# Sixteen-head attention: the four zero products of a half step, each on a column tile of 32, written as one product over the full array

## The chip, the cores and the metric

The kernel runs on one core of a Trainium2 chip. The metric is the device time of one execution in microseconds (us). The engines are named as in the profile: PE is TensorE (matrix products), PEld its weight loads, DVE is VectorE, ACT is ScalarE, POOL is GpSimd, SP issues DMAs. The profile also gives the TensorE clock that was granted, as a share of full speed.

## What is computed

A residual network of sixteen layers on `x` of shape (1, 2048, 128): in turn an attention or state-space layer and a feed-forward layer, each as `x = x + f(layernorm(x))`. The change touches the three layers of softmax attention with 16 heads of 8 columns:

```python
def heads(W, b):                       # 16 heads of 8
    y = jnp.einsum('btc,oc->bto', x, W) + b
    return y.reshape(B, T, H, D).transpose(0, 2, 1, 3)
att = jnp.einsum('bhqd,bhkd->bhqk', q, k) * (1.0 / np.sqrt(D))
att = jax.nn.softmax(att, axis=-1)     # L0_attn_b: after rope, and under a causal mask
y = jnp.einsum('bhqk,bhkd->bhqd', att, v)
return jnp.einsum('btc,oc->bto', y.transpose(0, 2, 1, 3).reshape(B, T, C), Wp) + bp
...
x = x + _L0_attn_b_ref(_layernorm(x, axis=-1), ...)   # stage Causal
...
x = x + _L2_attn_b_ref(_layernorm(x, axis=-1), ...)   # stage Attn2
...
x = x + _L3_attn_b_ref(_layernorm(x, axis=-1), ...)   # stage Filtered: q and k are filtered by a learned mask
```

## The kernel before

**Stages.** The layers are stages, one after the other: `CumSum, Moe0, Causal, Moe0, Mamba, Mla, Ssm, Moe2, Attn2, Moe2, Hale, Moe3, Filtered, Moe3`. While one stage ends, the first blocks of the next are fed in. A scheduler that goes by a simulated timeline orders the instructions of all stages up to Attn2; for the PE instructions of the 16-head stages it has no choice, because the helper `in_turn` stamps each of them with its place in the order of issue.

**Units.** `Causal`, `Attn2` and `Filtered` are of the class `Attn16`. The 2048 tokens are four blocks `b` of 512 queries, and the 16 heads are four groups `g` of four. A unit is a pair (g, b), so a stage has 16 units. For a unit there are two passes over the keys:

- `pass_a` finds the maximum of each query's scores. Line 829 multiplies 128 queries by 512 keys for two heads (`ps_a`, 128 x 1024), each head on a row tile of 32 rows; DVE takes the maximum over each row of 512 (line 833, `at_mx`). `set_max` puts the negated maxima into two spare rows of `q` (transposes of line 850, an ACT copy, a DMA).
- `pass_b` makes the scores the other way round. For each tile `kt` of 128 keys, in two halves `jj` of two heads each, line 900 multiplies keys by queries (row tiles of 32, `ps_b`), ACT takes the exponential (line 906, `at_P`), and `av` multiplies the values by it.

**The half step.** `pass_a` runs ahead of `pass_b`, and for each half `jj` PE gets, in this order: two products of line 829, two of line 900, and one call of `av`. I call this a half step. `av(kt, off, ps, half)` does one half of the query columns of tile `kt`, so the call in the first half step of a tile needs the exponentials of the tile before, and the second call needs nothing new. A stage without a mask has 512 half steps, `Causal` has 320 (keys beyond the diagonal are left out).

**The call of av.** `self.acc` (`ps_c`, one bank of PSUM) collects the output of the unit's four heads, each on 32 partitions. Line 879 is four products, one for each head `j`, of 128 rows and 32 columns of weights (`at_V`) on the column tile `32 * j`, with 256 columns of `at_P` in fp32; each shows in the trace as two matmul records (two passes). Then come the products with zeros (line 883):

```python
z = s if kt == 0 or end < BW else slice(half * BW // 2, (half + 1) * BW // 2)
for j in (3, 2, 1, 0):
    if not (kt == nkt - 1 and half):
        self.in_turn(nc.tensor.matmul(self.acc[32 * j : 32 * j + 32, z], c.zerob, c.wide[:, z], start=False, stop=False))
```

`zerob` is a constant tile of zeros (line 64), `wide` one of ones. The products add zero to `acc`. They have the same form as the value products, 128 rows on column tiles of 32, but are bf16. The last half step of a unit has none: 1296 of the 1344 half steps have four.

**Buffers.** `ps_a` has two buffers of two banks, `ps_b` three banks, `ps_c` one; these are the eight banks of PSUM. PE takes its instructions in order; the DMAs of these stages (maxima into `q`) go by SP's queue.

**The end of a unit.** After the last call of `av`, ACT copies `acc` to `at_u` (line 888). Every second unit ends with `tail` (transposes over the full array, line 922), and every fourth with `out` (transposes and the output product, lines 940 and 946). `prep` makes the next unit's `q` (line 760, row tiles) and once per block the projection for the next block's heads.

Of the kernel before, what the change touches and what calls it, by code (L numbers as in the profile page):

```python
# [15 lines left out]
BF16 = mybir.dt.bfloat16  # L16
# [5 lines left out]
P = 128  # L22
# [10 lines left out]
class Core:  # L33
    def __init__(self, ctx, tc, ins):
        self.ctx, self.tc, self.nc, self.ins = ctx, tc, tc.nc, ins
        nc = self.nc
        self.per = ctx.enter_context(tc.tile_pool(name="per", bufs=1))
        self.x = self.per.tile([P, NT, P], F32, name="x")
        self.load_x(ins["x"])
        self.ident = self.per.tile([P, P], F32, name="ident")  # L40
        make_identity(nc, self.ident)
        self.identb = self.per.tile([P, P], BF16, name="identb")
        nc.vector.tensor_copy(self.identb, self.ident)
        self.identr = self.per.tile([P, P], F32R, name="identr")
        nc.vector.tensor_copy(self.identr, self.ident)
        self.ones = self.per.tile([P, P], F32, name="ones")
        nc.vector.memset(self.ones, 1.0)
        self.nhalf = self.per.tile([P, 4], F32, name="nhalf")
        nc.vector.memset(self.nhalf, -0.5)
        self.rev8 = self.per.tile([P, 4, E], F32, name="rev8")  # L50
        for e in range(E):
            nc.vector.memset(self.rev8[:, :, e : e + 1], float(E - e))
        self.neg01 = self.load(self.per, "neg01", (P, 1), ins["neg01"])
        slots = self.per.tile([P, 4, P], F32R, name="slots")
        with tc.tile_pool(name="st0", bufs=1) as st:
            nc.vector.tensor_copy(slots, self.load(st, "slots_raw", (P, 4, P), ins["slots"]))
        self.slots = {"q": (slots[:, 0], slots[:, 1]), "k": (slots[:, 2], slots[:, 3])}
        self.kone = self.load(self.per, "kone", (P, 1), ins["kone"])
        one = self.per.tile([2, 1], F32R, name="ones2")
        nc.vector.tensor_copy(one, self.ones[0:2, 0:1])  # L60
        self.ones2 = one.to_broadcast([2, BW])
        self.wide = self.per.tile([P, BW], BF16, name="wide")
        nc.vector.memset(self.wide, 1.0)
        self.zerob = self.per.tile([P, 32], BF16, name="zerob")
        nc.vector.memset(self.zerob, 0.0)
        self.psum = ctx.enter_context(tc.tile_pool(name="psum", bufs=1, space=PSUM))
        self.shared = {}
# [617 lines left out]
class Attn16(Attention):  # L685
# [175 lines left out]
    def pass_b(self, u, scale):  # L861
        c, nc = self.c, self.c.nc
        g, b, i0, i1 = u
        self.turn_due(u)
        q, KT = self.qb[(g, b)], self.KT[g]
        nkt = 4 * b + i1 if self.causal else NT
        end = i1 * P

        def av(kt, off, ps, half):


            if kt == i0 == g % 2 == half == 0:
                self.acc = c.ps("c")
            mid = (off + end) // 2
            s = slice(mid, end) if half else slice(off, mid)
            for j in (3, 2, 1, 0):
                h = 27 * (4 * (g // 2) + j) + 9 * (g % 2)
                start, stop = kt == i0 == g % 2 == half == 0, kt == nkt - 1 and g % 2 == half == 1
                self.in_turn(nc.tensor.matmul(self.acc[32 * j : 32 * j + 32, s], self.V[:, kt, h : h + 32], ps[j][:, s], start=start, stop=stop))  # L879
            z = s if kt == 0 or end < BW else slice(half * BW // 2, (half + 1) * BW // 2)  # L880
            for j in (3, 2, 1, 0):
                if not (kt == nkt - 1 and half):
                    self.in_turn(nc.tensor.matmul(self.acc[32 * j : 32 * j + 32, z], c.zerob, c.wide[:, z], start=False, stop=False))  # L883
            if kt == nkt - 1 and half:
                self.closed = u
            if kt == nkt - 1 and g % 2 == half == 1:
                self.u = self.wk.tile([P, BW], F32, name="at_u", tag="at_t", bufs=2)
                nc.scalar.copy(self.u, self.acc)  # L888

        for kt in range(nkt):  # L890
            off = max(i0, kt - 4 * b) * P if self.causal else i0 * P
            diag = self.causal and kt >= 4 * b + i0
            ps = []
            for jj in range(2):
                self.pair = 1 - jj
                yield (kt + (jj + 1) / 2) / nkt
                pbs = [c.ps("b") for _ in range(2)]
                for k in range(2):
                    r = rows(2 * jj + k)
                    self.in_turn(nc.tensor.matmul(pbs[k][:, off:end], KT[r, kt * P : (kt + 1) * P], q[r, off:end], start=True, stop=not diag))  # L900
                if diag:
                    for k in range(2):
                        self.in_turn(nc.tensor.matmul(pbs[k][:, off : off + P], c.identb, self.maskbT, start=False, stop=True))
                for k in range(2):
                    p = self.wk.tile([P, BW], F32, name="at_P", bufs=self.NP)
                    nc.scalar.activation(p[:, off:end], pbs[k][:, off:end], AF.Exp, scale=scale)  # L906
                    ps.append(p)
                self.turn_due()
                self.later(1)
            self.late += [partial(av, kt, off, ps, half) for half in range(2)]  # L910
# [76 lines left out]
def rows(j):  # L987
    return slice(32 * j, 32 * j + 32)
# [1450 lines left out]
```

## Time and profile before

| | |
|---|---|
| median of 3 runs | 4835.98 us (4833.01 to 4851.77) |
| profiled execution | 4842.59 us, of which the span from first to last instruction is 4840.6 us |
| mean granted TensorE clock | 0.922 |
| PE, DVE, ACT busy | 91%, 77%, 63% of the span |
| half steps of Causal | from 345 to 855 us in the span, 1.60 us each on average |
| half steps of Attn2 | from 2214 to 2874 us, 1.29 us each |
| half steps of Filtered | from 3950 to 4617 us, 1.30 us each |
| records of line 883 | 5184 matmuls and 5184 weight loads |

The profile is one execution, so sums are held against its own 4842.59 us; the median lies 6.6 us lower. A matmul's recorded duration contains a part that overlaps with the next one, so costs are read from the distance between starts, not from durations.

### The profile page before, as it was taken

What the parts mean: (1) busy time and instruction counts of PE and PEld (TensorE: products, weight loads), DVE (VectorE), ACT (ScalarE), POOL (GpSimd) and SP (SyncE); (2) the same over time, 40 slices, a digit from 0 to 9 for tenths busy, and PEclk for the clock granted to TensorE, in tenths of its full rate; (3) what the DMA queues carried; (4) which work ended last, traced back from release to release, by engine and by line L of the source; (5) the groups of instructions that cost most, each with busy time, mean ns of one, the idle gap of its engine ahead of it and who ended that gap; (6) DMA issues with size and microseconds to landing.
All of it is one profiled execution on the core that took longest, in us unless ns stands there. A gap on an engine that the chain in (4) does not pass through costs nothing.

```text
span 4840.6 us, 89173 instructions
## 1 busy us (share of the span) xinstructions
PE 4411.5 (91%) x36388; PEld 2496.4 (52%) x36388; DVE 3713.6 (77%) x5694; ACT 3052.4 (63%) x5570; POOL 947.6 (20%) x826
## 2 busy tenths in 40 slices
PE   6979999988799998799999999989988989999998
PEld 4744444655344443463444457656656634444466
DVE  7867886689666653789999958457768879999777
ACT  4634667775355555356888875345546648888876
POOL 4730000544100000330000013012215600000056
PEclk9966899998699999888999999889998969999999
DMA  1010000000000000000000000112211000000000
GB/s 52 6 45 6 4 2 9 22 1 17 17 14 14 18 14 4 8 1 2 2 2 2 2 4 12 33 50 51 51 48 37 9 8 2 2 2 2 2 20 7
DMA packets 69484, 73.33 MB, mean 15 GB/s; under 512 B 17616, under 2 KB 44102, under 8 KB 69076
## 3 DMA queue, kind: packets, MB, share of 16 engines
q1 hardware_dynamic: 69076, 67.64, 5.0%
q8 instruction: 287, 4.70, 0.4%
q14 instruction: 121, 0.99, 0.1%
HBM read 32.09 MB, written 1.05 MB: 7 GB/s over the span
## 4 chain that ended last, share of the span: by engine, by line
PE 68%; DVE 21%; ACT 5%; issue 3%; POOL 2%; DMA 1%; SPq 0%; POOLq 0%; ACTq 0%; DVEq 0%
PE ps_c L879 15%; PE ps_a L829 10%; PE ps_c L1483 5%; DVE at_mx L833 4%; PE ps_b L900 4%; PE ps_a L1443 3%; PE ps_c L883 3%; PE ps_b L1496 3%; PE ps_b L148 2%; PE ps_a L148 2%; PE ps_a L150 2%; PE ps_b L149 2%; PE ps_a L149 2%; PE ps_b L150 2%; DVE m_hl L455 1%
## 5 line engine op out<-in xcount | busy, mean ns | idle before, releaser
L906 ACT ACTIVATE at_P<-ps_b 128x512 f32<-128x512 f32 (+2 forms) x2688 | 1414.4, 581 | 335.0 <-PE ps_b L900 211.1
L833 DVE TENSOR_REDUCE at_mx<-ps_a 128x2 f32<-128x1024 f32 (+2 forms) x1344 | 1537.7, 1184 | 106.5 <-PE ps_b L900 66.8
L879 PE MATMUL ps_c<-at_P,at_V 128*32 128x256 f32 (+3 forms) x10752 | 868.3, 396 | 7.8 <-ACT at_u L888 7.3
L900 PE MATMUL ps_b<-at_q,at_KT 32*128 32x512 f32 (+2 forms) x2688 | 759.5, 499 | 6.6 <-DMA at_q<-at_mT 5.0
L829 PE MATMUL ps_a<-at_KT,at_q 32*128 32x512 f32 (+3 forms) x2688 | 701.1, 521 | 48.0 <-DVE at_mx L833 45.7
L829 PEld LDWEIGHTS ps_a<-at_KT,at_q 32*128 32x128 f32 x2688 | 267.1, 196 | 497.4 <-issue 338.1
L1444 DVE TENSOR_REDUCE ml_mx<-ps_a 128x2 f32<-128x1024 f32 x256 | 305.4, 1222 | 216.4 <-PE ps_a L1443 215.4
L454 ACT ACTIVATE m_hh<-ps_a,moe_b 128x512 fp32r<-128x512 f32 x512 | 349.8, 689 | 189.1 <-DVE m_h L451 158.0
L455 POOL TENSOR_TENSOR m_hl<-m_h,m_hh 128x512 fp32r<-128x512 f32 x256 | 360.5, 1409 | 541.1 <-ACT m_hh L454 529.3
L1498 ACT ACTIVATE ml_P<-ps_b 128x512 f32<-128x512 f32 (+1 forms) x544 | 272.5, 576 | 231.8 <-PE ps_b L1496 229.7
L879 PEld LDWEIGHTS ps_c<-at_P,at_V 128*32 128x32 f32 x10752 | 215.8, 110 | 359.2 <-issue 181.0
L883 PE MATMUL ps_c<-wide,zerob 128*32 128x256 bf16 x5184 | 391.1, 282 | 0.0
L266 POOL TENSOR_TENSOR ln_rs<-ln_ve,nhalf 128x4 f32<-128x4 f32 x56 | 61.8, 1104 | 1650.3 <-DVE ln_ve L264 1641.4
L900 PEld LDWEIGHTS ps_b<-at_q,at_KT 32*128 32x128 f32 x2688 | 326.3, 189 | 73.5 <-issue 44.2
L455 DVE TENSOR_TENSOR m_hl<-m_h,m_hh 128x512 fp32r<-128x512 f32 x256 | 257.1, 1005 | 79.4 <-ACT m_hh L454 77.9
L453 ACT ACTIVATE m_h<-ps_a,moe_b 128x512 f32<-128x512 f32 x320 | 220.6, 690 | 77.1 <-DVE m_hl L455 42.0
L1483 PE MATMUL ps_c<-ml_P,ml_V 128*33 128x512 f32 (+3 forms) x1088 | 257.5, 596 | 2.9 <-ACT ml_P L1498 2.9
L148 PE MATMUL ps_b<-m_hh,moe_w2h 128*128 128x512 f32 x512 | 221.7, 433 | 20.7 <-DVE m_t L475 17.8
L149 PE MATMUL ps_b<-m_hl,moe_w2h 128*128 128x512 f32 x512 | 213.9, 418 | 26.4 <-DVE m_hl L455 20.7
L148 PE MATMUL ps_a<-ln_h,moe_w1h 128*128 128x512 f32 x512 | 218.7, 428 | 10.7 <-ACT m_hh L454 10.6
L883 PEld LDWEIGHTS <-zerob 128*32 128x32 bf16 x5184 | 156.1, 100 | 113.6 <-issue 10.8
L149 PE MATMUL ps_a<-ln_l,moe_w1h 128*128 128x512 f32 x512 | 207.4, 405 | 0.0
(655 smaller groups left out, 7759.7 us busy)
## 6 DMA issues: line engine op xcount, KB each, us to landing
hl_KS<-hl_pkh SPq DMA_DIRECT2D x160, 64.0 KB
moe_w_raw<-in_l0f_W SPq DMA_DIRECT2D x32, 256.0 KB
ml_pad<-ml_QT SPq DMA_DIRECT2D x32, 256.0 KB
moe_w_raw<-in_l3f_W SPq DMA_DIRECT2D x32, 256.0 KB
hl_KS<-hl_pkl SPq DMA_DIRECT2D x80, 64.0 KB
at_pad<-at_q SPq DMA_DIRECT2D x64, 64.0 KB
at_q<-at_mT SPq DMA_DIRECT2D x192, 4.0 KB
at_cosT<-in_cosT SPq DMA_DIRECT2D x8, 256.0 KB
```

The source lines that it names most:

```text
L148: nc.tensor.matmul(out, lh, rh, start=start, stop=False)
L149: nc.tensor.matmul(out, lh, rl, start=False, stop=False)
L454: nc.scalar.activation(hh, ph, AF.Relu, bias=bias)
L455: (nc.gpsimd if f in ((0, 2) if self.spare else MS) else nc.vector).tensor_tensor(hl, h, hh.bitcast(F32), ALU.subtract)
L829: self.in_turn(nc.tensor.matmul(pa[:, k, :w], q[r, i * P : (i + 1) * P], KT[r, ch * BW : ch * BW + w], start=True, stop=True))
L833: nc.vector.tensor_reduce(mx[:, i, 2 * jj : 2 * jj + 2, ch], pa[:, :, :w], AX.X, ALU.max)
L879: self.in_turn(nc.tensor.matmul(self.acc[32 * j : 32 * j + 32, s], self.V[:, kt, h : h + 32], ps[j][:, s], start=start, stop=stop))
L883: self.in_turn(nc.tensor.matmul(self.acc[32 * j : 32 * j + 32, z], c.zerob, c.wide[:, z], start=False, stop=False))
L900: self.in_turn(nc.tensor.matmul(pbs[k][:, off:end], KT[r, kt * P : (kt + 1) * P], q[r, off:end], start=True, stop=not diag))
L906: nc.scalar.activation(p[:, off:end], pbs[k][:, off:end], AF.Exp, scale=scale)
L1444: nc.vector.tensor_reduce(mx[:, i, :, ch], pa, AX.X, ALU.max)
L1483: self.in_turn(nc.tensor.matmul(self.acc[64 * j : 64 * j + m, s], v, ps[k][j][:, s], start=kt + k == 0, stop=kt + k == NT - 1))
```

## The change

The four products with zeros become one product with 128 columns of weights, over all 128 partitions of `acc` and the same query columns. The tile of zeros grows from 32 to 128 columns. It is for all three 16-head stages, since they share `pass_b`; `Hale` has its own `pass_b` without such products.

```diff
-        self.zerob = self.per.tile([P, 32], BF16, name="zerob")
+        self.zerob = self.per.tile([P, P], BF16, name="zerob")
         nc.vector.memset(self.zerob, 0.0)
...
             z = s if kt == 0 or end < BW else slice(half * BW // 2, (half + 1) * BW // 2)
-            for j in (3, 2, 1, 0):
-                if not (kt == nkt - 1 and half):
-                    self.in_turn(nc.tensor.matmul(self.acc[32 * j : 32 * j + 32, z], c.zerob, c.wide[:, z], start=False, stop=False))
+            if not (kt == nkt - 1 and half):
+                self.in_turn(nc.tensor.matmul(self.acc[:, z], c.zerob, c.wide[:, z], start=False, stop=False))
```

In the instruction streams PE loses 3 x 1296 matmuls and as many weight loads. The order of the other PE instructions within the half steps is as before. From Causal to Attn2 the scheduler exchanges some neighbouring instructions on DVE, ACT and POOL, and outside the half steps a few dozen on PE; SP's order is the same. The line numbers behind the change fall by one.

## The prediction

> **What bounds the kernel now.** I read the page first: where PE's clock falls, and what carries the chain.
>
> ```profile
> PEclk9966899998699999888999999889998969999999
> PE ps_c L879 15%; PE ps_a L829 10%; PE ps_c L1483 5%; DVE at_mx L833 4%; PE ps_b L900 4%; PE ps_a L1443 3%; PE ps_c L883 3%; PE ps_b L1496 3%; PE ps_b L148 2%; PE ps_a L148 2%; PE ps_a L150 2%; PE ps_b L149 2%; PE ps_a L149 2%; PE ps_b L150 2%; DVE m_hl L455 1%
> L883 PE MATMUL ps_c<-wide,zerob 128*32 128x256 bf16 x5184 | 391.1, 282 | 0.0
> ```
>
> The zero products are on the chain (3%), and never wait. The clock is low in slices 3 and 4 (Causal) and where stages change. Then the timeline inside Filtered, two half steps at full clock:
>
> ```profile
> 4400.79 0.64 PE L879 MATMUL ps_c<-at_P,at_V 128*32 128x256 f32 x8
> 4400.93 2.19 ACT L906 ACTIVATE at_P<-ps_b 128x512 f32<-128x512 f32 x4 [0.19 <-PE ps_b L900]
> 4401.25 0.29 PE L883 MATMUL ps_c<-wide,zerob 128*32 128x256 bf16 x4
> 4401.47 0.18 PEld L829 LDWEIGHTS ps_a<-at_KT,at_q 32*128 32x128 f32 x2 [0.32 <-issue]
> 4401.48 0.59 PE L900 MATMUL ps_b<-at_q,at_KT 32*128 32x512 f32 x2
> 4402.07 0.16 PEld L879 LDWEIGHTS ps_c<-at_P,at_V 128*32 128x32 f32 x8 [0.31 <-ACT at_P L906]
> 4402.53 0.29 PE L883 MATMUL ps_c<-wide,zerob 128*32 128x256 bf16 x4
> 4402.75 0.49 PE L829 MATMUL ps_a<-at_KT,at_q 32*128 32x512 f32 x2
> ```
>
> The value products start at 4400.79, zeros .46 later, scores .22 after that. The first half step, 4400.37 to 4401.48, is PE alone: 1.11 us. In the second, L879 waits for ACT until 4402.07 (PE was ready .43 after 4401.47, so .17 are slack), and ACT's first exponential had waited for PE (.19). So two half steps are one ring of 2.39: scores on PE, ACT until 4402.07, then values and zeros, 0.68. Only one of two zero groups lies in it. DVE's maxima follow PE.
>
> **What a zero product costs, and a change of tile shape.** The timeline again, at a unit's end, where there are no zeros, and at other changes of shape:
>
> ```profile
> 2253.85 0.64 PE L879 MATMUL ps_c<-at_P,at_V 128*32 128x256 f32 x8
> 2254.41 0.50 PE L829 MATMUL ps_a<-at_KT,at_q 32*128 32x512 f32 x2
> ```
> ```profile
> 3252.65 0.29 PE L2144 MATMUL ps_b<-hl_am,hl_V 128*32 128x128 f32 x4
> 3252.88 0.49 PE L2157 MATMUL ps_a<-hl_QP,hl_KS 128*128 128x512 f32 x1
> ```
> ```profile
> 3081.53 0.28 PE L1929 MATMUL ps_b<-at_mc,identb 128*128 128x256 bf16 x1
> 3081.74 0.43 PE L1918 MATMUL ps_c<-at_P,at_V 128*32 128x64 f32 x16
> ```
>
> From values to scores takes .56 without zeros and .68 with: the four cost .11, one stream of 256 columns (.107), so they run side by side. Without zeros the values take .10 longer until the scores than until zeros (.56 against .46): this is the price of leaving the column tiles. The other pairs price it with the full array. Four column products (.107 of stream, the last starting .02 after the first) are followed by a full one .225 after the first start: .10 for the change. A full bf16 product of 256 columns, the new product's very form, is followed by column tiles .21 later: .107 and .10. Leaving the full array for row tiles costs the same (last L922 to L900: .202, with .107 of stream). At half clock it is .14 (L922 to L900 .350, with .213 of stream).
>
> **Part 1: PE's half step.** Removed: four products (.11, and .02 of staggered starts). Added: one product (.11) and a second change of shape, since columns now go to full and full to rows (.10). Its 128 columns of weights can't load before the change: two full bf16 products of 128 columns after one (L903, starts .065 apart, .053 of stream) show .012 for that. Sum: +.10 (range −.02, if the change is free, to +.13), per half step at full clock; +.14 at half clock.
>
> The Trainium skill (TensorE: Matmul & The Clock Gate, section LDWEIGHTS (loading the stationary operand)) counts a weight load as its columns / 1.2 in ns: .107 here, and if all of it showed, Part 1 would be +.20. The row of L903 speaks against that.
>
> **Part 2: full clock, Attn2 and Filtered.** The ring holds one product of two: 2.39 + .10 = 2.49. PE's own two half steps become 2.42, still below. So +.10 per pair, 2 x 256 pairs: +53. If unit ends kept PE late throughout it would be 1024 x .10 = 105. ACT and DVE only gain slack.
>
> **Part 3: Causal.** 248 half steps start at full clock, 1.39 on average, so many wait for other things (its chain is 17% DVE); I take half of them at .10: +13. The 72 at half clock are mostly PE's: 72 x .14 = +10.
>
> **Part 4: the clock.** This is the term with the most in it. The trace's clock moves in steps of 3.41 us. The timeline and the windows at a slow spell:
>
> ```profile
> 4158.56 0.44 PE L883 MATMUL ps_c<-wide,zerob 128*32 128x256 bf16 x4
> 4158.93 0.79 PE L829 MATMUL ps_a<-at_KT,at_q 32*128 32x512 f32 x2
> 4159.66 1.08 PE L879 MATMUL ps_c<-at_P,at_V 128*32 128x256 f32 x8
> 4160.89 0.59 PE L829 MATMUL ps_a<-at_KT,at_q 32*128 32x512 f32 x2
> ```
> ```profile
> 4157.70:4161.10 3.40, 3.40 (x34) 1.25 (x32) 1.72 (x5) 2.17 (x4) 0.00 (x0) 0.50 0.03 8
> 4161.10:4164.50 3.40, 3.40 (x51) 1.40 (x51) 3.09 (x8) 2.78 (x6) 0.00 (x0) 1.00 0.00 0
> ```
>
> At half clock a saturated half step is 1.96 (4158.93 to 4160.89). Its streams are scores .43 (512 columns; full products of that length, such as L1443's, start .43 apart at half clock), values .85 (two passes, 4159.66 to the zeros .85 later), zeros .21 (twice .107): 1.49, or 76%; the rest is changes and weight loads. I summed streams so for every 3.41 us window of the trace at half clock (rows and column tiles of 32 weighted as their share of the array). Of 132 windows below 65%, 1 was the last of its slow spell; of 35 from 65 to 75%, 7; of 55 above 75%, 53. PE without a wait is not enough: 3949.50 to 3952.90 is all PE, has 74%, and stayed slow. The spells begin after windows under 40% (with one exception), in these stages at unit ends.
>
> After, streams stay and the half step becomes 2.09: 71%; depending on phase a window holds 65 to 75%, against 73 to 82% before. So a slow spell ends in one of five windows instead of nearly each.
>
> The same page (Part 1, the table of the two states) lets one busy window of some 3.4 us bring the full clock back. By it PE is busy before and after, Part 4 is zero and the sum 4919. The window at 3949.50, busy throughout and still slow after it, speaks against reading "busy" as "without a wait".
>
> Attn2 and Filtered have 5 spells of 9 windows together; at five windows each 25. A slow window loses 40% (2.09 against 1.25), so 16 x 3.41 x .40 = +22; four times longer spells +124. Causal has 8 spells with 49 of the 58 slow windows of these stages, and its rate of 8 ends in 49 windows falls: five of the ends came from the six windows above 75%, which now pass one time in five, and of the other three ends, in windows that lose 5 points too, I leave one or two. At 2 or 3 in 49 the spells would run into one another until the projections (eight full products of 512 columns, once a block) end them. At half clock a half step there takes 2.29 against 1.39, some of it other work; I take .7 for each of the 248, and two fifths of them: +69; bounds 0 and 174.
>
> **At nothing.** The wider zero tile is one memset at the start beside the loads of `x`, smaller than that of `wide` next to it. The exchanged instructions outside the half steps keep their count, so I set them at 0, with 10 either way.
>
> **Sum.** 53 + 13 + 10 + 22 + 69 = +167 on the profiled 4842.6 is 5010; the median lies 6.6 lower: 5003.
>
> **Rivals.**
> - *Drains only.* The clock recovers as before. Against it: the counts above; for it: my shares are modelled, and the limit could be 70%. 53 + 23 = 76 (up to 128 with PE late): 4912.
> - *Locked clock.* If 75% is a hard limit and 71% never passes, slow spells last for stages: 512 x (2.09 − 1.30) twice, and 174 + 10 in Causal: some +990, 5830. Against it: 7 of 35.
> - *Faster: the change of shape is free.* Full and column tiles both use 128 rows; if that is no change, .02 and three weight loads less per half step: at most 1296 x .02 = 26: 4810. It decides if L882 to L829 and L879 to L882 stay at .20 each. Against it: L2144 to L2157.
> - *Fewer falls.* A later PE lets DVE and ACT run ahead, and the lulls that start spells vanish: 58 windows x 3.41 x .36 = −71 against +76: 4841. Against: lulls are transposes that wait for `at_u`.
>
> **The numbers.** Forecast (4930 to 5262, with bounds 105 + 23 + 124 + 174 at the top) 66%; drains only (4885 to 4930) 15%; locked 13%; no change 4% (fewer falls); faster 2%. The range 4885 to 5330 leaves most of the locked case, no change and faster out. About 0.5%, 24 us, is what a measurement can tell from no change: faster .02, same .04, slower .94.
>
> **What would show it.** L879's last start to L882 .31 (was .20 to L883); L882 to L829 .21; the pair of half steps 2.49; at half clock 2.09; more and longer runs of half clock in slices 3 to 7, 18 to 23 and 33 to 38. I am wrong if the first is .20, or if the clock's mean stays 0.92 with the time above 4930.

## The result, and the profile after

The changed kernel takes 4957.08 us (median of 4 runs, 4948.14 to 4968.90) against 4835.23 us before: the ratio is 1.024, with a 95% interval of 1.0219 to 1.0261. The forecast was 5003 with a range of 4885 to 5330: the direction is right, and the loss is 122 us where 167 were expected. The profiled execution took 4953.05 us with a span of 4951.0, so 110.4 us more span than before, at a mean granted clock of 0.914 (0.922 before).

The page of the changed kernel: the engines' busy time, the clock by slices, the chain by line, and the two groups of the new product (line 882).

```profile
PE 4528.3 (91%) x32481; PEld 2431.6 (49%) x32500; DVE 3747.4 (76%) x5694; ACT 3052.3 (62%) x5570; POOL 945.3 (19%) x826
PEclk9965879998699999888999999889989979999999
PE ps_c L879 15%; PE ps_a L829 10%; PE ps_c L882 5%; PE ps_c L1482 5%; DVE at_mx L833 4%; PE ps_a L1442 3%; PE ps_b L899 3%; PE ps_b L1495 3%; PE ps_b L148 2%; PE ps_a L148 2%; PE ps_a L150 2%; PE ps_a L149 2%; PE ps_b L149 2%; DVE m_hl L455 2%; PE ps_b L150 2%
L882 PEld LDWEIGHTS <-zerob 128*128 128x128 bf16 x1296 | 124.7, 96 | 556.4 <-issue 555.5
L882 PE MATMUL ps_c<-wide,zerob 128*128 128x256 bf16 x1296 | 378.1, 292 | 0.0
```

The zero product's share of the chain went from 3% to 5%, though there is one product instead of four. The clock is lower in slices 4 and 6, which lie in Causal.

The timeline of the changed kernel in Filtered, at full clock (start, length, engine, line, operation, tiles, count, and the wait in brackets):

```profile
4428.24 0.64 PE L879 MATMUL ps_c<-at_P,at_V 128*32 128x256 f32 x8
4428.38 2.08 ACT L905 ACTIVATE at_P<-ps_b 128x512 f32<-128x512 f32 x4 [0.18 <-PE ps_b L899]
4428.81 0.49 PE L829 MATMUL ps_a<-at_KT,at_q 32*128 32x512 f32 x2
4428.81 0.71 PE L899 MATMUL ps_b<-at_q,at_KT 32*128 32x512 f32 x2
4429.51 0.16 PEld L879 LDWEIGHTS ps_c<-at_P,at_V 128*32 128x32 f32 x8 [0.31 <-ACT at_P L905]
4429.51 0.64 PE L879 MATMUL ps_c<-at_P,at_V 128*32 128x256 f32 x8
4430.08 0.28 PE L882 MATMUL ps_c<-wide,zerob 128*128 128x256 bf16 x1
4430.30 0.50 PE L829 MATMUL ps_a<-at_KT,at_q 32*128 32x512 f32 x2
4430.73 0.64 PE L879 MATMUL ps_c<-at_P,at_V 128*32 128x256 f32 x8
4430.87 0.60 ACT L905 ACTIVATE at_P<-ps_b 128x512 f32<-128x512 f32 x1 [0.41 <-PE ps_a L829]
```

This is the end of a unit, so the call of `av` at 4428.24 has no zeros. From the values to the zero product it is .57 now (.46 before), and from there to line 829 still .22. ACT's group of exponentials starts every 2.49 (4428.38 to 4430.87), against 2.39. The same at half clock, one half step:

```profile
4242.65 1.08 PE L879 MATMUL ps_c<-at_P,at_V 128*32 128x256 f32 x8
4243.67 0.39 PE L882 MATMUL ps_c<-wide,zerob 128*128 128x256 bf16 x1
4243.99 0.79 PE L829 MATMUL ps_a<-at_KT,at_q 32*128 32x512 f32 x2
4244.72 1.08 PE L879 MATMUL ps_c<-at_P,at_V 128*32 128x256 f32 x8
```

4242.65 to 4244.72 is 2.07 (1.96 before): the zero product starts 1.02 after the values (.85 before), and line 829 .32 later.

Where the 110.4 us are, by stage. First the kernel before, then the changed one: window, its length, busy time and instructions of PE, PEld, DVE, ACT and POOL, then the granted clock, the DMA share and GB/s. The rows are Causal, Attn2 and Filtered, from the first to the last half step.

```profile
345.00:855.00 510.00, 491.62 (x5460) 224.97 (x5463) 387.75 (x555) 323.92 (x681) 9.25 (x18) 0.84 0.02 6
2214.00:2874.00 660.00, 652.00 (x8228) 287.51 (x8220) 582.52 (x608) 570.21 (x1064) 5.28 (x6) 0.99 0.01 2
3950.00:4617.00 667.00, 650.73 (x8216) 284.78 (x8219) 581.20 (x600) 573.67 (x1064) 4.30 (x4) 0.99 0.01 2
```
```profile
347.00:897.00 550.00, 538.79 (x4545) 216.45 (x4537) 392.69 (x550) 323.89 (x681) 9.24 (x18) 0.79 0.02 5
2254.00:2944.00 690.00, 679.25 (x6731) 255.30 (x6727) 597.80 (x608) 571.64 (x1064) 5.28 (x6) 0.99 0.01 2
4021.00:4724.00 703.00, 688.59 (x6731) 255.67 (x6728) 595.95 (x600) 572.53 (x1064) 4.30 (x4) 0.98 0.01 2
```

To a tenth, from the half steps' starts: Causal +40.8, Attn2 +30.5, Filtered +35.8, and 3.3 elsewhere. Attn2 lost its 30 us at an unchanged clock of 0.99; Causal lost its 41 together with clock, 0.84 to 0.79. ACT's busy time did not change, so all of it is time in which ACT waits more.

### The profile page after: what moved, and what is told of

It reads as the page before. It is cut to its first block, busy times and chain, and to the rows that moved or that the text cites. A ratio compares the mean times of both kernels' runs of the same rounds, so it can differ in the third digit from the quotient of the medians.

```text
span 4951.0 us, 81380 instructions
## 1 busy us (share of the span) xinstructions
PE 4528.3 (91%) x32481; PEld 2431.6 (49%) x32500; DVE 3747.4 (76%) x5694; ACT 3052.3 (62%) x5570; POOL 945.3 (19%) x826
## 3 DMA queue, kind: packets, MB, share of 16 engines
HBM read 32.09 MB, written 1.05 MB: 7 GB/s over the span
## 4 chain that ended last, share of the span: by engine, by line
PE 68%; DVE 21%; ACT 4%; issue 3%; POOL 2%; DMA 1%; SPq 0%; POOLq 0%; ACTq 0%; DVEq 0%
PE ps_c L879 15%; PE ps_a L829 10%; PE ps_c L882 5%; PE ps_c L1482 5%; DVE at_mx L833 4%; PE ps_a L1442 3%; PE ps_b L899 3%; PE ps_b L1495 3%; PE ps_b L148 2%; PE ps_a L148 2%; PE ps_a L150 2%; PE ps_a L149 2%; PE ps_b L149 2%; DVE m_hl L455 2%; PE ps_b L150 2%
## 5 line engine op out<-in xcount | busy, mean ns | idle before, releaser
L833 DVE TENSOR_REDUCE at_mx<-ps_a 128x2 f32<-128x1024 f32 (+2 forms) x1344 | 1573.8, 1186 | 153.4 <-PE ps_b L899 94.1
L879 PE MATMUL ps_c<-at_P,at_V 128*32 128x256 f32 (+3 forms) x10752 | 882.2, 402 | 8.0 <-ACT at_u L887 7.6
L899 PE MATMUL ps_b<-at_q,at_KT 32*128 32x512 f32 (+2 forms) x2688 | 721.5, 505 | 5.8 <-DMA at_q<-at_mT 5.0
L882 PEld LDWEIGHTS <-zerob 128*128 128x128 bf16 x1296 | 124.7, 96 | 556.4 <-issue 555.5
L882 PE MATMUL ps_c<-wide,zerob 128*128 128x256 bf16 x1296 | 378.1, 292 | 0.0
L899 PEld LDWEIGHTS ps_b<-at_q,at_KT 32*128 32x128 f32 x2688 | 284.9, 191 | 49.6 <-issue 15.1
L453 ACT ACTIVATE m_h<-ps_a,moe_b 128x512 f32<-128x512 f32 x320 | 220.5, 689 | 78.5 <-DVE m_hl L455 40.8
```

The lines of the kernel that those rows point to most:

```text
L833: nc.vector.tensor_reduce(mx[:, i, 2 * jj : 2 * jj + 2, ch], pa[:, :, :w], AX.X, ALU.max)
L882: self.in_turn(nc.tensor.matmul(self.acc[:, z], c.zerob, c.wide[:, z], start=False, stop=False))
```

## The experiments

Two theories stood against each other for the size of the loss. **Shape**: the second change of tile shape costs .10 us in the ring of two half steps, and that is all. **Shape and clock**: besides, PE's stream becomes a smaller share of each window, and half clock lasts longer. A *window* is one of the 3.41 us steps in which the clock moves, a *spell* is a stretch of windows at half clock, and a *fall* is where a spell begins. *Stream* is the time in which columns of queries or keys pass through the array, *drain* the time that PE loses at a change of shape. All edits but those marked otherwise are made to the kernel before, where `zerob` has 32 columns. The zero products add nothing to `acc`, so leaving out or doubling them changes no output.

### A full product with 16 query columns

Made to the changed kernel: both changes of shape stay, the stream of the zero product all but goes.

```diff
-                self.in_turn(nc.tensor.matmul(self.acc[:, z], c.zerob, c.wide[:, z], start=False, stop=False))
+                t = slice(z.start, z.start + 16)
+                self.in_turn(nc.tensor.matmul(self.acc[:, t], c.zerob, c.wide[:, t], start=False, stop=False))
```

> The one product over the full array keeps its place, but takes only 16 query columns instead of 256 (it adds zero to fewer columns). Theory (each change of tile shape costs .10 us of PE at full clock, and a slow spell of the clock ends only after a 3.41 us window with a share of streams near 75%): from the last value product to the scores .31 + .12 = .43 instead of .42 before, so at full clock the pair of half steps stays 2.39 and the unmasked stages lose nothing there; but at half clock the streams are 1.29 of 1.96 us, 66%, and slow spells run on: 4950 to 5250, about 5030, granted clock under .90. Rival (the clock goes by PE without a wait, and only PE's time counts): as before, 4835 to 4850, clock .92. Rival (one product less work, shape change free): 4780.

Measured: 4945.91 against 4837.94, ratio 1.0228 (1.0205 to 1.0252), just under the expected 4950 to 5250, with the clock below .90 as expected. Its timeline in Filtered, and its window of Causal:

```profile
4401.95 0.64 PE L879 MATMUL ps_c<-at_P,at_V 128*32 128x256 f32 x8
4402.52 0.18 PE L883 MATMUL ps_c<-wide,zerob 128*128 128x16 bf16 x1
4402.63 0.49 PE L829 MATMUL ps_a<-at_KT,at_q 32*128 32x512 f32 x2
```
```profile
344.00:920.00 576.00, 562.19 (x4546) 234.53 (x4544) 392.14 (x553) 324.72 (x681) 9.24 (x18) 0.68 0.02 5
```

The product's stream is .007 (16 of the 256 columns that take .107), yet it holds PE for .11: that is the change of shape, with whatever part of the weight loads waits for it. The median pair of half steps at full clock is 2.400, .01 above the 2.389 of before. So this kernel pays the change of shape and saves the stream, and is level at full clock; it is slower by 2.3% nearly all through the clock (0.891 over the span, 0.68 in Causal).

### No zero products at all

```diff
-            for j in (3, 2, 1, 0):
-                if not (kt == nkt - 1 and half):
-                    self.in_turn(nc.tensor.matmul(self.acc[32 * j : 32 * j + 32, z], c.zerob, c.wide[:, z], start=False, stop=False))
```

> The kernel before without any zero products. Theory: PE's half step is .11 shorter, the ring of two half steps 2.28 instead of 2.39, -28 us in each unmasked stage and -13 in Causal; at half clock the streams are 1.28 of 1.74 us, 73.5%, where 5 to 8 of 13 to 18 windows ended a spell, so spells grow a little, most in Causal (+20): 4790 (4760 to 4830). Rival (75% is a hard limit and without zeros the clock stays down): above 5000. Rival (PE is not the bound; ACT and DVE set the pace): 4835.

Measured: 4880.90 against 4837.94, ratio 1.0101 (1.0077 to 1.0126): slower, where a gain was expected. Its clock by slices and its three stages:

```profile
PEclk9965567998789999797999999989998959899999
```
```profile
345.00:911.00 566.00, 547.45 (x4223) 215.88 (x4215) 392.61 (x550) 322.77 (x679) 9.26 (x18) 0.65 0.02 5
2274.00:2916.00 642.00, 629.41 (x6221) 245.89 (x6220) 570.28 (x608) 555.67 (x1062) 5.30 (x6) 0.97 0.01 2
3991.00:4652.00 661.00, 641.53 (x6228) 248.65 (x6227) 570.03 (x600) 562.18 (x1065) 4.31 (x4) 0.95 0.01 2
```

The gain at full clock came as expected: the median pair is 2.280, and Attn2 is 16 us shorter than before from its first to its last half step. But Causal is 58 us longer, because its clock fell from 0.84 to 0.65. The zero products that add nothing to the result pay for themselves by keeping the clock. "Shape" has no place for this.

### The four products twice

```diff
-            for j in (3, 2, 1, 0):
+            for j in (3, 2, 1, 0, 3, 2, 1, 0):
```

> The kernel before with the four zero products on column tiles done twice: .107 us more of stream per half step, where the changed kernel has .105 more without stream. Theory: the pair of half steps becomes 2.49 as in the changed kernel (+27 us in each unmasked stage), Causal +13 at full clock and +15 at half clock, but the share of streams at half clock rises from 76 to 79% and spells are no longer than before: 4895 (4870 to 4915); the distance to the changed kernel, some 60 us, is the clock's. Rival (the changed kernel's loss is all PE time): as the changed kernel, 4957. Rival (zero products are hidden): 4835.

Measured: 4888.73 against 4837.94, ratio 1.0102 (1.0085 to 1.0120), as expected, with the highest clock of all kernels here, 0.933. Its stages:

```profile
347.00:847.00 500.00, 482.55 (x6681) 242.70 (x6680) 389.64 (x551) 323.51 (x682) 9.25 (x18) 0.92 0.02 7
2206.00:2899.00 693.00, 680.98 (x10198) 324.48 (x10200) 599.45 (x608) 572.30 (x1065) 5.29 (x6) 0.99 0.01 2
3973.00:4656.00 683.00, 677.72 (x10198) 323.37 (x10201) 597.58 (x600) 572.44 (x1064) 4.31 (x4) 1.00 0.01 2
```

This is the clean pair to the changed kernel: a second group of four costs the ring as much as the change of shape (median pair 2.499 and 2.494; Attn2 693 and 690.5), but it is stream, not drain. Causal at 0.92 is 10 us shorter than before; in the changed kernel it is 41 us longer. At equal cost on the path, the clock separates the two.

### The full product in the unmasked stages only

Made to the changed kernel; Causal has its four column products back.

```diff
+                if self.causal:
+                    for j in (3, 2, 1, 0):
+                        self.in_turn(nc.tensor.matmul(self.acc[32 * j : 32 * j + 32, z], c.zerob[:, 0:32], c.wide[:, z], start=False, stop=False))
+                else:
...
```

> The full product in Attn2 and Filtered only, column tiles as before in Causal. Theory: the two stages lose what they lost in the changed kernel, 30 + 36, and Causal is as before, 510 us from its first to its last half step: 4901 (4885 to 4920). Rival (the 41 us of Causal come from the scheduler's exchanges or from where the clock's windows fell, not from its own products): up to 4957.

Measured: 4909.34 against 4837.94, ratio 1.0147 (1.0132 to 1.0163), as expected. Its Causal stage takes 506.3 us, as before, and Attn2 and Filtered 692.9 and 704.2, as in the changed kernel. So the loss adds up by stages: some 70 us are the unmasked ones, and the other 40 to 50 are Causal.

### Only one of the two calls without zeros

Which of the two zero groups of a pair lies on the ring? Two kernels, both with Causal as before: the unmasked stages without zeros in the first call of a tile (`half == 0`), and in the second.

```diff
-                if not (kt == nkt - 1 and half):
+                if not (kt == nkt - 1 and half) and (self.causal or half == 1):
```

In the other kernel the last condition is `half == 0`.

> The kernel before, in Attn2 and Filtered without the zeros of the first call of av for a tile of keys (half 0), the one whose value products wait for ACT. Theory (a ring of scores, two pairs of exponentials, values and the zeros of this call sets the pace): the ring loses .11 us per pair of half steps, -28 us in each of the two stages, less some 10 for longer slow spells of the clock: 4793 (4780 to 4805). Rival (PE's own sum of both half steps sets the pace): the same here as without the zeros of the second call.

> The kernel before, in Attn2 and Filtered without the zeros of the second call of av (half 1), which needs nothing new. Theory: these zeros lie beside ACT's exponentials, so the pair of half steps stays 2.39 and nothing is gained; slow spells of the clock are somewhat longer: 4845 (4832 to 4855), some 50 above the kernel without the zeros of the first call. Rival (PE's own sum sets the pace): -28 us in each of the two stages here too, 4793.

Measured: without the first 4813.90 against 4841.91, ratio 0.9947 (0.9931 to 0.9964); without the second 4845.41, ratio 1.0017 (1.0005 to 1.0028). The second call's zeros are off the path: leaving out 480 groups of them gained nothing (median pair 2.392), and the expected 4845 came. The first call's are on it, but gave .066 per pair (2.389 to 2.323) where .11 was expected, so the time lies above the expected 4780 to 4805. The timeline of the kernel without them, in Filtered, PE and then ACT:

```profile
4423.22 0.64 PE L879 MATMUL ps_c<-at_P,at_V 128*32 128x256 f32 x8
4423.79 0.51 PE L829 MATMUL ps_a<-at_KT,at_q 32*128 32x512 f32 x2
4423.80 0.70 PE L900 MATMUL ps_b<-at_q,at_KT 32*128 32x512 f32 x2
4424.43 0.64 PE L879 MATMUL ps_c<-at_P,at_V 128*32 128x256 f32 x8
4424.89 0.29 PE L883 MATMUL ps_c<-wide,zerob 128*32 128x256 bf16 x4
4425.11 0.50 PE L900 MATMUL ps_b<-at_q,at_KT 32*128 32x512 f32 x2
```
```profile
4423.36 2.09 ACT L906 ACTIVATE at_P<-ps_b 128x512 f32<-128x512 f32 x4 [0.24 <-PE ps_b L900]
4425.68 0.60 ACT L906 ACTIVATE at_P<-ps_b 128x512 f32<-128x512 f32 x1 [0.23 <-PE ps_b L900]
```

The two score products of line 900 at 4423.80 take .70 together instead of .49: in the trace the second starts at 4424.01, when a semaphore of ACT frees its bank of `ps_b`, .65 after the exponential of 4423.36 began. From there it is .42 to the second call's values (4424.43), .68 through values and zeros to the next scores (4425.11), and .57 until ACT starts again (4425.68): .65 + .42 + .68 + .57 = 2.32, the measured 2.323. So there is a second ring, through the three banks of `ps_b`, .07 shorter than the first, and it holds the other call's zeros. Without any zeros it is .11 shorter again, and the first ring decides with 2.28, as the kernel without zeros showed.

### One product with 8 columns of weights

Made to the changed kernel, to see what the 128 columns of weights cost.

```diff
-                self.in_turn(nc.tensor.matmul(self.acc[:, z], c.zerob, c.wide[:, z], start=False, stop=False))
+                self.in_turn(nc.tensor.matmul(self.acc[0:8, z], c.zerob[:, 0:8], c.wide[:, z], start=False, stop=False))
```

> The changed kernel with 8 columns of zero weights instead of 128 (zeros are added to 8 partitions only); the product stays outside the column tiles. Theory (the price is the change of tile shape, not the weights, and the clock goes by rows in use): starts .31 and .21 us as in the changed kernel, 4957 (4940 to 4975). Rival (the load of 128 columns of weights costs the .10): .20 and .20 or so, 4850. Rival (the clock goes by all cells in use, rows and columns): full clock as the changed kernel, slow spells as with 16 query columns or longer: 5010.

Measured: 4853.91 against 4841.91, ratio 1.0027 (1.0016 to 1.0038). Its timeline and its Causal stage:

```profile
4400.00 0.64 PE L879 MATMUL ps_c<-at_P,at_V 128*32 128x256 f32 x8
4400.48 0.27 PE L882 MATMUL ps_c<-wide,zerob 128*8 128x256 bf16 x1
4400.68 0.50 PE L829 MATMUL ps_a<-at_KT,at_q 32*128 32x512 f32 x2
```
```profile
347.00:857.00 510.00, 489.99 (x4553) 216.60 (x4552) 387.01 (x553) 324.03 (x681) 9.23 (x18) 0.84 0.02 6
```

The premise did not hold: from the last value product to the zeros it is .215, not .31, so a product of 8 columns stays in the shape of the column tiles, and the run says nothing on the weights of the full one. It says two other things. Without the change of shape the loss is gone, with one product as with four. And one product of 8 columns keeps Causal's clock at 0.84, as four with 128 together do: the clock does not go by how many columns of the array work.

### One product with 64 columns

Made to the changed kernel: `self.acc[0:64, z]` and `c.zerob[:, 0:64]`.

> The changed kernel with 64 columns of zero weights instead of 128 (zeros are added to 64 partitions). The kernel with 8 columns kept the column tiles' pace (.215 from the last value product, no .31), so it did not tell the change of shape from the weight load. Theory (any other tile shape costs .10 at each change, whatever its weights; the clock goes by rows and time): starts .31 and .21 us, the pair of half steps 2.49, 4957 (4940 to 4975). Rival (the load of the weights costs it): half of the price, starts .25 and .20, about 4900. Rival (no change of shape between tiles of 32 and 64 columns): .215 and .20, 4850.

Measured: 4996.65 (4973.68 to 5014.70) against 4845.41, ratio 1.0312 (1.0278 to 1.0346), above the expected 4940 to 4975. The profile is of the fastest of the four executions.

```profile
4399.89 0.64 PE L879 MATMUL ps_c<-at_P,at_V 128*32 128x256 f32 x8
4400.46 0.30 PE L882 MATMUL ps_c<-wide,zerob 128*64 128x256 bf16 x1
4400.69 0.49 PE L829 MATMUL ps_a<-at_KT,at_q 32*128 32x512 f32 x2
```

From the last value product to the zeros it is .309, as with 128 columns: so 64 columns are a shape of their own too, and pay the change; the .25 of the rival by which half the weights cost half did not come. The load itself is not shorter in the trace, though (108 ns on average against 96), so this run does not part the change of shape from the load that waits for it. To line 829 it is .226, against .212 with 128 columns. Half as many columns of weights are slightly dearer, the median pair is 2.508 against 2.494, and the kernel with them is slower than the changed one. The .014 explain some 7 us of that; the rest was not followed.

### Zeros where they pay

The first experiments say that Causal wants more zeros and the unmasked stages fewer. Twice in Causal, and none in the first call of the other stages:

```diff
-            for j in (3, 2, 1, 0):
+            for j in (3, 2, 1, 0, 3, 2, 1, 0) if self.causal else (3, 2, 1, 0) if half else ():
```

> A version that may beat both, on column tiles: in Causal the four zero products twice, in Attn2 and Filtered only in the second call of av, whose place in the ring was shown free. Theory: Causal -5 to -10 as in the kernels with zeros twice, the two stages -17 and -15 as without the zeros of the first call: 4805 (4795 to 4820), .993 of the kernel before. Rival (the gain of the two stages hangs on where the clock's windows fall): 4815 to 4840.

Measured: 4819.37 against 4845.41, ratio 0.9949 (0.9933 to 0.9966). Twice in Causal, and in the other stages only for the first four tiles of keys (`if kt < 4`):

> A version that may beat both, on column tiles: in Causal the four zero products twice, in Attn2 and Filtered only in the calls for the first 4 of 16 tiles of keys, where slow spells that start at a unit's end are still open. Theory: Causal 500 us as with zeros twice (-10), the two stages lose .11 us per pair for three quarters of their calls (-21 each), their spells stay as before: 4784 (4770 to 4805). Rival (spells also start or stay open later in a unit): clock as without zeros, 4800 to 4820.

Measured: 4827.35 against 4841.91, ratio 0.9973 (0.9956 to 0.9990). Both beat both kernels, by under 1% and less than expected: in the profiles Attn2 and Filtered are 17 us shorter each in the first and 8 and 13 in the second, where half clock in these two stages rose from 28.6 to 47.8 us. Causal is only 7 and 2 us shorter. There half clock falls from 167 to 85 and 94 us, but a half step at full clock becomes dearer, 1.46 to 1.47 against 1.395. The gain in Causal is hardly more than its spread: with two groups it took 500, 502 and 508 us in three kernels, with one group 510 in the kernel before and 506 to 507 in three others. Of the first one's 42 us in the stages, 17 came back outside the half steps (the span is 24.5 us shorter), a third of it between Attn2 and Filtered; what came late there was not followed. Leaving out the first call's zeros alone (0.9947) is as good; the two are not told apart.

## Why the prediction was right, and where its sizes were off

**Part 1, the half step: right.** From the last value product to the zeros .311 (predicted .31, .196 before), on to line 829 .212 (predicted .21). So the four products' stream is replaced by an equal one, and one change of shape is added: .10. At half clock it is .11, where .14 was predicted (the saturated half step goes from 1.96 to 2.07). That the wider weights can't load before the change shows too: the load of the zeros starts .307 after the last value product's start, and .002 after it before the change, so the .10 holds what is exposed of the load. The Trainium skill (TensorEngine Tiling (Array Packing), section Key Properties) says that changing the mode of tiling drains TensorE, and gives no figure; the .10 here is one.

**Part 2, the ring: right.** 2.494 for the pair (predicted 2.49). Half steps that start at full clock became .059 and .061 longer in Attn2 and Filtered; with some 500 in each that is 60 us, where 53 were predicted. About half of the 7 on top lies in the first pair of each unit, which became .21 longer (3.22 to 3.43): there PE is late through both calls, as the bound of 105 allowed. The other half was not followed. That only one of the two groups lies on the ring was shown by leaving out each in turn; that a second ring is only .07 behind was not seen in the prediction, and it would have spoilt a gain of .10, though not this loss.

**Part 3, Causal without the clock: 15 instead of 23.** The 248 half steps at full clock gave 3 (1.395 to 1.410), not 13: they wait for other things even more than half the time. The 72 at half clock gave 12 (2.29 to 2.46, times 72), predicted 10; this is a difference of means over different half steps, and by the saturated .11 it would be 8.

**Part 4, the clock: right in kind, too large.** This is the term that was mis-sized. In Causal 24 more half steps ran at half clock, each 1.05 longer than one at full clock (2.46 against 1.41): +25, where 99 more (two fifths of 248) and +69 were predicted. In the other two stages half clock rose from 28.6 to 45.1 us, which cost about 6, where 22 were predicted. Together 31 of 110, instead of 91 of 167, so the result lies near the lower end of the forecast's 4930 to 5262; the 3 us outside the stages lie within the 10 either way. The sign named for being wrong, a mean clock that stays at 0.92, did not come: it is 0.909 to 0.915 in the four executions of the changed kernel, and 0.917 to 0.927 in all executions of the kernel before.

The rule behind it held. Counted as before, in the changed kernel 2 of 149 windows at half clock with under 65% of stream ended a spell, 9 of 47 with 65 to 75%, and 44 of 51 above; the forecast of one in five for the middle band is what came. One weight in the count was wrong, though: columns do not count by their share of the array. In the kernel with one product of 8 columns the three stages have 57 windows at half clock. With a column tile counted as a quarter of the array none of them is above 75%, yet 12 of 15 from 65 to 75%, and 3 of 42 below, ended a spell. Counted as the time in which any column streams, it is 13 of 13 above, 2 of 13 between and none of 31 below. Counted by that time in the traces of all twelve kernels, 596 of 712 windows above 75% ended a spell, 85 of 550 between, and of 1633 below only the 12 with which the executions end.

What failed was the step from the saturated half step to Causal's windows: I let five of Causal's eight ends fall away because a saturated half step goes from 76 to 71%. But it goes to 72% (2.07, not 2.09), and most of Causal's slow windows are not saturated (26 of 49 were under 65% already), so they had nothing to lose. The windows above 75% became 4 instead of 6, not one or two. By time of streaming, those from 65 to 75% became 31 instead of 18, and six of the seven spells ended there: 7 ends in some 70 windows, where 2 or 3 in 49 were predicted.

Nor had I asked what sets how often the clock falls. Divided by the number of spells, Causal's time at half and at full clock shows both ends:

| zero products of a half step | us at half clock | spells | us of one spell | us at full clock between falls |
|---|---|---|---|---|
| none | 400 | 9 | 44 | 19 |
| full, 16 query columns | 371 | 9 | 41 | 23 |
| four column tiles (before) | 167 | 8 | 21 | 43 |
| one of 8 columns | 162 | 10 | 16 | 35 |
| 64 columns | 258 | 7 | 37 | 43 |
| full (the change) | 236 | 7 | 34 | 45 |
| four, twice | 75 | 6 | 13 | 71 |

The last column goes by the stream that a half step has at full clock: none or nearly none of zeros, 19 to 23; one group in any form, 35 to 45; two, 71. The traces show why: the clock falls after a window at full clock with little stream. Counted by time of streaming in all twelve kernels, 670 of the 693 windows after which it fell had less than 40%, and only 86 of the 13361 other windows at full clock did, none of them under 35%. The change leaves that stream alone, so the clock falls as often as before (45 against 43), and only the spells grow, from 21 to 34 us. This also answers the miss in the run without zeros: its expectation counted the ring and spells that grow a little; they doubled (21 to 44 us), and the falls, which it did not count, came every 19 us. The numbers are of one execution of each kernel, with 6 to 10 spells in it, so a row is good for its order of size; the Causal of before, in three other kernels with the same four products, had 156 to 160 us at half clock and falls every 43 to 50, and with two groups, in the two kernels above, 85 and 94 us and falls every 70 and 52.

**The rivals.** *Drains only* (4912; the 4919 named beside the page is the same 76 us on the profiled execution): most of the loss, 75 of 110 us (60, 3 and 12), is drains, but the clock's part is real: the kernel with the same ring and double stream has a ratio of 1.010 where the changed one has 1.024, and the run with the full product in the unmasked stages alone gives Causal its 41 us back. *Locked clock* (5830): no, 71 to 72% still passes. *Free change of shape* (4810): the run with 16 columns excludes it. *Fewer falls* (4841): no, the clock fell as often.

**Open.** Where the limit between 65 and 75% lies, and what besides the share decides there: in the changed kernel one spell has three windows, at 67, 70 and 75%, all without a wait on PE (3.40 of 3.40 us busy), and the clock rose after the third:

```profile
4241.90:4245.30 3.40, 3.40 (x24) 1.09 (x24) 1.13 (x4) 1.52 (x3) 0.00 (x0) 0.50 0.01 4
4245.30:4248.70 3.40, 3.40 (x26) 0.99 (x18) 2.54 (x6) 1.73 (x4) 0.00 (x0) 0.50 0.00 0
4248.70:4252.10 3.40, 3.40 (x26) 0.90 (x22) 2.58 (x4) 2.12 (x4) 0.00 (x0) 0.50 0.02 5
```

The Trainium skill (TensorE: Matmul & The Clock Gate, Part 1) lets one busy window suffice; the first two of these do not fit it, if busy means that PE does not wait. Whether rows count by their share was not tested: all zero products here have 128.

## What to carry to other kernels

A product between others of another tile shape costs the change of shape on both sides, .10 us each here at full clock, however little it streams, so look at the shape of the neighbours before merging tiles. Where PE's clock is at stake, count per window the time in which PE streams: time in which PE drains looks busy in a profile and holds up no clock, while a product that computes nothing can pay for itself in a stage that waits, and costs in one that does not. Before crediting a gain on a ring, look for the second ring: here it was .07 of 2.39 behind.

## What the runs showed of the hardware

- A product of 128 rows and 8 columns, streaming 256 columns, keeps the clock as four products on all 128 columns do (162 and 167 us at half clock in Causal, mean clock over the span 0.920 and 0.922).
- Products of 64 columns after column tiles of 32 pay the same change of shape as full ones (.309 and .311), and one of 8 columns pays none (.215).
- A product with 64 columns of weights is followed .226 later, one with 128 columns .212, and its weight load takes 108 ns in the trace on average, that with 128 columns 96. The Trainium skill (TensorEngine Tiling (Array Packing), section Restrictions) says that column tiling excludes the fast loading of weights; the direction agrees, the size is .014. No run separates this cause from others.
